# A four-layer Mamba image network on one core: B, C and step sizes of a segment from one projection, and another end for the last image

## The chip, the cores and the metric

The kernel runs on one core of a Trainium2 chip. The metric is the device time of one execution in microseconds (us); the time before is the median of three runs. Engines are named as in the profile: PE is TensorE (PEld its weight loads), DVE is VectorE, ACT is ScalarE, POOL is GpSimd, SP is SyncE, which here only issues DMAs. [...]

## The reference

Four images of 64 x 64 pixels (4096 tokens each) with 96 channels pass four layers. Each layer is a mixer and a feed-forward network, both with a residual, behind layer norms. The mixer of layer 0 is a gated scan; those of layers 1 to 3 are a selective scan in four directions (rows, columns, and both backwards), with 192 channels, 16 states and step sizes of rank 6. What matters here, cut from one of them:

```python
xc = silu(depthwise_conv(x @ in_proj_w.T ...))           # 192 channels
xs = stack([rows, columns, rows backwards, columns backwards])
x_dbl = einsum('bkdl,kcd->bkcl', xs, x_proj_w)            # 6 + 16 + 16 numbers per token
dts, Bs, Cs = split(x_dbl, [R, R + N], axis=2)            # step sizes, B, C
delta = softplus(einsum('bkrl,kdr->bkdl', dts, dt_w) + dt_b)
h = exp(delta * A) * h + delta * u * B                    # per channel and state, over 4096 tokens
y = sum over states of h * C, plus Ds * u                 # then the four directions are added,
out = (layer_norm(y) * silu(z)) @ out_proj_w.T            # normalised, gated and projected
```

The feed-forward network quantises its operands to eight bits and its sums to f16: `relu(q(x W1 + b1))`, then `W2`.

## The kernel before

**Scans.** Layers 1 to 3 of the four images are twelve stages, run one after the other (`scans`). A stage has two directions in time (d), four segments of 1024 tokens in each, and three chunks of 128 partitions (64 channels of each of two orders, rows and columns). Every chunk has 16 states, so a stage has 384 tiles of 128 x 1024 and the kernel 4608. A tile k with state n goes through all engines in a fixed order that the program writes out: SP broadcasts the row of C from a DRAM scratch (`c_rows`, c <- cs); ACT makes the decay (`decays`, da); PE broadcasts the row of B into two PSUM banks (`b_rows`, bc <- bs, sel); DVE multiplies it by du in place (bc <- du, bc) and scans (h <- da, carry, bc); POOL multiplies by C (`times_c`, c <- h, c), one tile later; PE adds the states up in PSUM (`accumulate`, acc), three tiles later. B is needed as bf16 for that broadcast and is kept as three bf16 parts, 32 rows each, that add up to the f32 number; `sel` adds them.

**What runs beside.** Between a tile's DVE product and its scan the program calls `beside`, which advances three generators by a step each: the preparation of the next chunk (`prepare_chunk`: dt_proj, softplus, delta, du), that of the next segment (`next_segment`, `prepare_segment`), and the job of the next stage, the work between two scans of an image (`between`: joining the orders, norm, gating, out_proj, feed-forward, and, for the next layer, norm, in_proj and convolution in strips of 512 tokens). A generator yields where it wants a tile's pause; `yield True` asks for a free bank, and is held up while none is free. There are two single banks (tag `ps`), shared by all three. A `Job` advances by a credit of `rate` steps per tile: 1.65 for a job that the next stage needs, 2.6 for the ends of the first three images, which run in the last two stages. Each engine executes its instructions in the order in which the program issued them (`InOrder`).

**`prepare_segment`** begins at tile n = 4 of a segment's chunk 1, for the next segment. For both halves of 512 columns it projects u (three matmuls over the three chunks) to 108 rows: B three times, rows 0 to 95, and the 12 step-size rows. ACT copies the step sizes to `rows` and B to bf16 in `bs`, 96 rows at once. DVE takes the remainder, `rem = ps - bs`, from PSUM, again 96 rows, and ACT writes rows 32 to 95 of it as bf16 into `bs`. POOL then subtracts the second part from rows 64 to 95, which leaves the third. After that a second projection of the same u, with 32 columns of weights, makes C (x_proj_c), which ACT copies over `rows[0:32]`, and SP stores it to `cs`. The step sizes must be there when chunk 2 begins, else the program drains the segment's generator at that place (`sg.steps`); all of it must be there at n = 13 of chunk 2.

**Norms.** A layer norm's inverse root is Exp(-0.5 Ln(v)), refined by five small POOL instructions. Ln and Exp lie in different tables of ACT. A norm that has been measured is put on `pending`; `logarithms()` takes all of those at once. In a job it is called when no generator can go on for `patience` steps.

**The last image's end** runs alone behind the scans: `Job(between(images[-1], 3, dst), patience=1).finish()`, at the rate of 1.4, on the two single banks. Eight strips pass join (y_t, four joins of eight program matmuls), mixer (y_c, out_proj) and feed-forward (ff_xt, ff_h, ff_y).

Lines: `wide` and `bank` 117 to 128, `Job` 708 to 738, `prepare_segment` 763 to 809, `beside` and the tile loop 985 to 1050, pools and jobs 1285 to 1303, the weights' layout 1335 to 1355. In the trace nearly every instruction is on line 78, the wrapper that keeps the order, so it is read by tile names.

Of the kernel before, what the change touches and what calls it, by code (L numbers as in the profile page):

```python
# [10 lines left out]
F32 = mybir.dt.float32  # L11
# [4 lines left out]
ALU = mybir.AluOpType  # L16
# [5 lines left out]
NS = 16  # L22
DI = 192
R = 6
HID = 4 * C
T = 1024
MM = 512
# [9 lines left out]

NB3 = 96
NC2 = 2 * NS
XPW = NB3 + 2 * R + NC2  # L40
W_IN = 0
W_OUT = W_IN + 6 * 128
W_CW = W_OUT + 2 * C
# [5 lines left out]
W_XP = W_LN + 4  # L49
W_SSM = W_XP + 6 * XPW  # L50

# [48 lines left out]
def metaformer(ctx: ExitStack, tc: tile.TileContext, x, l0_ab, l0_rest, ssm, ffn, out):  # L100
    nc = tc.nc
    pe, act, dve, pool, sp = (
        InOrder(tc, e) for e in (nc.tensor, nc.scalar, nc.vector, nc.gpsimd, nc.sync)
    )
# [4 lines left out]
    pbc = ctx.enter_context(tc.tile_pool(name="pbc", bufs=2, space=bass.MemoryType.PSUM))  # L109

    def sb(bufs, tag, shape, dtype=F32):
        return pools[bufs].tile(shape, dtype, tag=tag, name=tag)

    def const(name, shape, dtype=F32):
        return pools[1].tile(shape, dtype, name=name)

    def wide():
        return pbc.tile([128, T], F32, tag="bc", name="bc")


    banks = {"free": 2, "back": 0}

    def bank(name):
        banks["free"] -= 1
        return pbc.tile([128, MM], F32, tag="ps", name=name)

    def release():
        banks["back"] += 1

    def settle():  # L130
        banks["free"] += banks["back"]
        banks["back"] = 0
# [27 lines left out]
    for k in range(2):  # L160
        p = slice(64 * k, 64 * k + 64)
# [9 lines left out]
    for n in range(NS):  # L171
        for k in range(2):
            at = NS * k + n
# [19 lines left out]
    for layer in range(4):  # L193
# [8 lines left out]
        b = const(f"b_{layer}", [128, 3 + C])  # L202
# [35 lines left out]
    pending = []  # L238
# [36 lines left out]
    class Weights:  # L275
# [17 lines left out]
        def load_xp(self):  # L293
            if self.xp is None:
                self.xp = sb(1, "xp", [128, 6 * XPW])
                sp.dma_start(out=self.xp, in_=ssm[self.layer - 1, :, W_XP:W_SSM])
# [411 lines left out]
    class Job:  # L708
# [23 lines left out]
                    logarithms()  # L732
                    self.waited = 0

        def finish(self):
            while not self.done:
                self.step()
                settle()


# [22 lines left out]
    def prepare_segment(item, sg):  # L763

        xp = weights[item.layer].xp
        m = NB3 + 2 * R

        def project(ps, a, b, k):

            for c in range(3):  # L770
                o = (3 * item.d + c) * XPW
                cols = slice(k * MM, (k + 1) * MM)
                pe.matmul(
                    ps[0 : b - a],
                    xp[:, o + a : o + b],
                    sg.us[c][:, cols],
                    start=c == 0,
                    stop=c == 2,
                )
                if c:  # L780
                    yield

        sg.rows = sb(1, "rows", [128, T])
        for k in range(2):
            cols = slice(k * MM, (k + 1) * MM)
            ps = bank("x_proj_b")
            yield from project(ps, 0, m, k)

            bs = sg.bs[:, cols]
            act.copy(sg.rows[NB3:m, cols], ps[NB3:m])  # L790
            sg.steps = k == 1
            act.copy(bs, ps[0:NB3])
            yield
            rem = sg.rows[0:NB3, cols]
            dve.tensor_tensor(rem, ps[0:NB3], bs, ALU.subtract)
            release()
            yield
            for p in (32, 64):
                act.copy(bs[p : p + 32], rem[p : p + 32])
            yield k == 0  # L800
        pool.tensor_tensor(sg.bs[64:96], sg.rows[64:96], sg.bs[64:96], ALU.subtract)
        for k in range(2):
            cols = slice(k * MM, (k + 1) * MM)
            yield True
            ps = bank("x_proj_c")
            yield from project(ps, m, m + NC2, k)
            act.copy(sg.rows[0:NC2, cols], ps[0:NC2])
            release()
        sp.dma_start(out=sg.cs, in_=sg.rows[0:NC2])

    def prepare_chunk(item):

# [37 lines left out]
    def next_segment(items):  # L850

        sg = load_segment(items[0])
        for i in items:
            i.sg = sg
        yield
        yield
        yield True
        yield from prepare_segment(items[0], sg)

    def scans(stages, jobs, pac):  # L860
# [11 lines left out]
        for i in items[:3]:  # L872
            i.sg = sg
        drain(Chain(prepare_segment(items[0], sg), True))
        drain(Chain(prepare_chunk(items[0]), True))
        tiles = [(i, n) for i in items for n in range(NS)]
# [27 lines left out]
        def b_rows(k):  # L904
            i, n = tiles[k]
            b = live[k, "b"] = wide()
            for half in range(2):
                cols = slice(half * MM, (half + 1) * MM)
                pe.matmul(
                    b[:, cols], sel[:, n, :], i.sg.bs[:, cols], start=True, stop=True  # L910
                )
# [138 lines left out]
    def gated(images, job, pac):  # L1050
# [134 lines left out]
        def project(t):  # L1185

            st, i = t["st"], t["i"]
            t["ab"] = wide()
            for kind in range(2):
                pe.matmul(  # L1190
                    t["ab"][:, kind * MM : (kind + 1) * MM], block(kind, i), st.xn, start=True, stop=True
                )
# [92 lines left out]
    images = [Image() for _ in range(NB)]  # L1285
    for i, im in enumerate(images):
        im.src = x[i * L : (i + 1) * L, :]
        im.dst = out[i * L : (i + 1) * L, :]
    with tc.tile_pool(name="pl0", bufs=1, space=bass.MemoryType.PSUM) as pl0:
        gated(images, Job(between(images[0], 0), 2.6, patience=1), pl0)  # L1290
    stages = [(im, layer) for layer in range(1, 4) for im in images]
    jobs = []
    for at in range(len(stages)):
        jobs.append([])
        if at + 1 < len(stages):
            im, layer = stages[at + 1]
            jobs[-1].append(Job(between(im, layer - 1), 1.65))

        for im in {10: images[:2], 11: images[2:3]}.get(at, ()):
            jobs[-1].append(Job(between(im, 3, im.dst), 2.6))  # L1300
    with tc.tile_pool(name="pac", bufs=1, space=bass.MemoryType.PSUM) as pac:
        scans(stages, jobs, pac)
    Job(between(images[-1], 3, images[-1].dst), patience=1).finish()

# [24 lines left out]
def _chunks(v):  # L1331

    v = v.reshape(2, 2, DI, -1)
    v = [np.concatenate([v[:, o, c : c + 64] for c, o in halves], 1) for halves in CHUNKS]
    return np.stack(v, 1).transpose(2, 0, 1, 3)


def _scan(in_w, conv_w, conv_b, xp_w, dt_w, dt_b, A_logs, Ds, ln_w, ln_b, out_w):
    w = np.zeros((128, W_SSM), np.float32)
    twice = np.r_[128:DI, 128:DI]  # L1340

    xp = np.zeros((128, 2, 3, XPW), np.float32)
    m = NB3 + 2 * R
    for d in range(2):
        for chunk, halves in enumerate(CHUNKS):
            for k, (ch, order) in enumerate(halves):
                t = xp_w[2 * d + order].T[ch : ch + 64]
                v = xp[64 * k : 64 * k + 64, d, chunk]
                for s in range(3):
                    v[:, 32 * s + NS * order : 32 * s + NS * order + NS] = t[:, R : R + NS]  # L1350
                v[:, NB3 + R * order : NB3 + R * order + R] = t[:, :R]
                v[:, m + NS * order : m + NS * order + NS] = t[:, R + NS :]
    w[:, W_XP:W_SSM] = xp.reshape(128, -1)
    t = in_w.T
    w[:C, W_IN : W_IN + 448] = np.concatenate([t[:, :128], t[:, twice], t[:, DI:]], 1)
    dt = np.zeros((2 * R, 2, 3, 128), np.float32)
    for d in range(2):
        for chunk, halves in enumerate(CHUNKS):
            for k, (ch, order) in enumerate(halves):
                t = dt_w[2 * d + order].T  # L1360
                dt[R * order : R * order + R, d, chunk, 64 * k : 64 * k + 64] = t[:, ch : ch + 64]
    w[NB3 : NB3 + 2 * R, W_IN:W_OUT] = dt.reshape(2 * R, -1)
    w[:, W_OUT : W_OUT + C] = out_w.T[:128]
    w[:64, W_OUT + C : W_CW] = out_w.T[128:]
    taps = conv_w.reshape(DI, 9)
    w[:, W_CW : W_CW + 9] = taps[:128]
    w[:64, W_CW + 9 : W_CB] = np.concatenate([taps[128:, 0:3], taps[128:, 6:9]], 1)
    w[64:, W_CW + 9 : W_CW + 12] = taps[128:, 3:6]
    w[:, W_CB:W_DTB] = np.stack([conv_b[:128], conv_b[twice]], 1)
    w[:, W_DTB:W_AL] = _chunks(dt_b[..., None]).reshape(128, -1)  # L1370
    w[:, W_AL:W_DS] = _chunks(A_logs.reshape(4, DI, NS)).reshape(128, -1)
    w[:, W_DS:W_LN] = _chunks(Ds.reshape(4, DI, 1)).reshape(128, -1)
    w[:, W_LN : W_LN + 2] = np.stack([ln_w[:128], ln_b[:128]], 1)
    w[:64, W_LN + 2 : W_XP] = np.stack([ln_w[128:], ln_b[128:]], 1)
    return w
# [46 lines left out]
```

## Time and profile before

| | us |
|---|---|
| median of three runs | 19681.59 |
| lowest and highest of them | 19680.81, 19689.28 |
| the profiled execution's own time | 19688.32 |
| span of its profile | 19686.5 |
| of that: layer 0, to the first scan of layer 1 | 1817.2 |
| scans of layers 1 to 3 | 17576.5 |
| end of the last image, behind the last scan | 292.8 |
| mean granted clock of PE | 0.815 of full |

Busy over the span: DVE 90%, PE 83%, POOL 79%, ACT 62%. Times in the profile are from the start of the span. "Idle before" is the time an engine stood still ahead of an instruction, with what ended it: `DVE bc <- PE bc` means that the DVE product of a tile waited for the PE broadcast into its tile. A PE matmul of the program with f32 operands is two records in the trace. A view of windows gives each engine's busy time in a stretch, in the order PE, PEld, DVE, ACT, POOL, and the granted clock of PE; a timeline gives start, duration, engine and operation.

### The profile page before, as it was taken

The numbers are of one execution on the slowest core, as the hardware profiler recorded it, in microseconds if no ns is written. First come the engines' busy times: TensorE is split into PE (matmuls) and PEld (weight loads), VectorE is DVE, ScalarE is ACT, GpSimd is POOL, SyncE is SP. The second block draws the span as 40 slices with busy tenths as digits, with TensorE's granted clock in tenths as the row PEclk, the third lists the DMA queues.
The fourth block names the chain that finished last, engine by engine and source line by source line (L and its number), as shares of the span: only waits on it lengthen the run. The fifth ranks groups of instructions, "written<-read, shape, count | busy, mean of one in ns | idle before, by whom it ended". The sixth has DMA issues, their size and how long they took to land. (4 is left out here: it accounts for less than half of the span.)

```text
span 19686.5 us, 224801 instructions
## 1 busy us (share of the span) xinstructions
PE 16267.7 (83%) x70400; PEld 4750.9 (24%) x70400; DVE 17666.9 (90%) x13768; ACT 12256.8 (62%) x19331; POOL 15495.8 (79%) x10086
## 2 busy tenths in 40 slices
PE   8998787787888887787887888787888888888876
PEld 3332121121122222222222222222222222222223
DVE  6757999999999999999999999999999999998884
ACT  4544665665665665665666666666666666666664
POOL 3435888888888888888888888888888888878884
PEclk9998787787887797797797787797887787787886
DMA  2213676666676667666666676666666666676663
GB/s 52 50 48 87 169 185 168 170 187 164 171 189 173 166 184 182 168 185 178 170 188 176 170 186 172 170 188 174 171 186 172 170 189 174 171 187 169 165 176 89
DMA packets 1269876, 3192.65 MB, mean 162 GB/s; under 512 B 440336, under 2 KB 440560, under 8 KB 1262544
## 3 DMA queue, kind: packets, MB, share of 16 engines
q1 hardware_dynamic: 1268688, 3178.27, 61.5%
q8 instruction: 568, 9.31, 0.2%
q14 instruction: 620, 5.08, 0.1%
HBM read 2818.81 MB, written 308.28 MB: 159 GB/s over the span
## 5 line engine op out<-in xcount | busy, mean ns | idle before, releaser
L78 POOL TENSOR_TENSOR c<-h,c 128x1024 f32<-128x1024 f32 (+1 forms) x4992 | 11334.8, 2277 | 3377.8 <-DVE h L78 1478.0
L78 DVE TENSOR_TENSOR_SCAN h<-da,carry,bc 128x1024 f32<-128x1024 f32 x4608 | 10795.4, 2343 | 530.3 <-POOL c L78 17.0
L78 PE MATMUL acc<-c,twice 64*64 64x512 f32 x36864 | 6215.7, 751 | 20.1 <-POOL c L78 20.0
L78 ACT ACTIVATE da<-delta,decay 128x1024 f32<-128x1024 f32 x4608 | 5280.9, 1147 | 1491.5 <-DVE h L78 1475.6
L78 DVE TENSOR_TENSOR bc<-du,bc 128x1024 f32<-128x1024 f32 x4608 | 5565.6, 1208 | 488.4 <-PE bc L78 461.6
L78 PE MATMUL bc<-bs,sel 96*128 96x512 bf16 x9216 | 3384.4, 455 | 2343.3 <-DVE h L78 2235.9
L78 ACT COPY carry<-h 128x1 f32<-128x1 f32 x3456 | 649.5, 188 | 3374.5 <-DVE h L78 3368.7
L78 PEld LDWEIGHTS <-sel 96*128 96x128 bf16 x9216 | 552.2, 101 | 7301.0 <-DVE h L78 5519.2
L78 PEld LDWEIGHTS acc<-c,twice 64*64 64x64 f32 x36864 | 1130.7, 153 | 2799.4 <-issue 1860.2
L78 ACT ACT_TABLE_LOAD x1155 | 1481.9, 1283 | 36.5 <-DVE mv L78 20.3
L78 PE MATMUL conv<-pad,tap_lo 128*128 128x512 f32 x1728 | 906.5, 634 | 0.0
L78 PE MATMUL dt_proj<-rows,w 12*128 12x512 f32 x1152 | 826.5, 804 | 6.4 <-ACT delta L78 6.4
L78 ACT ACTIVATE du<-e,ones 128x1024 f32<-128x1024 f32 x576 | 659.3, 1145 | 199.3 <-POOL delta L78 194.5
L78 POOL TENSOR_TENSOR delta<-delta,du 128x1024 f32<-128x1024 f32 x288 | 679.8, 2361 | 72.0 <-ACT du L78 70.3
L78 PE MATMUL x_proj_b<-u,xp 128*108 128x512 f32 x1152 | 687.6, 713 | 46.4 <-DMA xp<-in_ssm 15.5
L78 PE MATMUL x_proj_c<-u,xp 128*32 128x512 f32 x1152 | 642.0, 672 | 76.1 <-ACT rows L78 67.0
L78 POOL TENSOR_TENSOR e<-e,du 128x1024 f32<-128x1024 f32 x288 | 679.8, 2360 | 2.4 <-ACT du L78 2.4
L78 ACT ACTIVATE c<-c,l_bias 128x512 f32<-128x512 f32 x384 | 263.6, 686 | 670.5 <-PE c L78 665.9
L78 POOL TENSOR_TENSOR du<-delta,u 128x1024 f32<-128x1024 f32 x288 | 680.4, 2363 | 0.1
L78 POOL TENSOR_TENSOR delta<-delta,e 128x1024 f32<-128x1024 f32 x288 | 678.8, 2357 | 0.1
L78 PE MATMUL conv<-pad,tap_hi 128*128 128x512 f32 (+1 forms) x1152 | 601.8, 624 | 0.6 <-ACT u L78 0.5
L78 DVE TENSOR_TENSOR_SCAN h<-da,l_carry,bc 128x512 f32<-128x512 f32 x384 | 491.4, 1280 | 41.9 <-DVE bc L78 2.3
(152 smaller groups left out, 15200.8 us busy)
## 6 DMA issues: line engine op xcount, KB each, us to landing
c<-cs SPq DMA_DIRECT2D x9216, 256.0 KB, 4.2
u<-u SPq DMA_DIRECT2D x288, 512.0 KB, 6.7
y<-y SPq DMA_DIRECT2D x1152, 128.0 KB, 3.2
y<-y SPq DMA_DIRECT2D x144, 512.0 KB, 6.8
xr<-x SPq DMA_DIRECT2D x224, 192.0 KB, 5.1
u<-u SPq DMA_DIRECT2D x288, 128.0 KB, 3.6
pad<-y SPq DMA_DIRECT2D x288, 128.0 KB, 4.9
z<-zl SPq DMA_DIRECT2D x96, 256.0 KB, 2.0
```

Of the source, the lines that this page charges most:

```text
L78: ins = f(*a, **k).ins
```

## The change

**In a segment's preparation** there is one projection to 108 rows: B in rows 0 to 31, C in 32 to 63, zeros in 64 to 95, step sizes in 96 to 107. ACT copies all 108 rows from PSUM to `rows`, then the first part of B, 32 rows, to bf16, and the bank is released. Two steps later DVE takes the remainder of the 32 rows from `rows` and `bs`, both in SBUF, into `rows[64:96]`; ACT copies it to `bs` twice; POOL makes the third part as before. C goes from `rows[32:64]` to DRAM. The second projection and its two copies are gone.

**Job rate**: 1.58 in place of 1.65 for jobs that the next stage needs.

**The last image's end**: the two wide PSUM tiles (four banks) come from a pool of their own that is closed behind the scans. The end then has six single banks, a rate of 3, and `eager=True`: `logarithms()` is called after every step that left something pending.

```diff
-XPW = NB3 + 2 * R + NC2
+XPW = NB3 + 2 * R
...
-        def finish(self):
+        def finish(self, eager=False):
             while not self.done:
                 self.step()
+                if eager and pending:
+                    logarithms()
                 settle()
...
     def prepare_segment(item, sg):
         xp = weights[item.layer].xp
-        m = NB3 + 2 * R
-        def project(ps, a, b, k):
-            for c in range(3):
-                o = (3 * item.d + c) * XPW
-                cols = slice(k * MM, (k + 1) * MM)
-                pe.matmul(ps[0 : b - a], xp[:, o + a : o + b], sg.us[c][:, cols], ...)
-                if c:
-                    yield
-        sg.rows = sb(1, "rows", [128, T])
+        rows = sg.rows = sb(1, "rows", [128, T])
         for k in range(2):
             cols = slice(k * MM, (k + 1) * MM)
-            ps = bank("x_proj_b")
-            yield from project(ps, 0, m, k)
+            ps = bank("x_proj")
+            for c in range(3):
+                o = (3 * item.d + c) * XPW
+                pe.matmul(ps[0:XPW], xp[:, o : o + XPW], sg.us[c][:, cols], ...)
+                if c:
+                    yield
             bs = sg.bs[:, cols]
-            act.copy(sg.rows[NB3:m, cols], ps[NB3:m])
+            act.copy(rows[0:XPW, cols], ps[0:XPW])
             sg.steps = k == 1
-            act.copy(bs, ps[0:NB3])
-            yield
-            rem = sg.rows[0:NB3, cols]
-            dve.tensor_tensor(rem, ps[0:NB3], bs, ALU.subtract)
+            act.copy(bs[0:32], ps[0:32])
             release()
             yield
+            yield
+            rem = rows[64:96, cols]
+            dve.tensor_tensor(rem, rows[0:32, cols], bs[0:32], ALU.subtract)
+            yield
             for p in (32, 64):
-                act.copy(bs[p : p + 32], rem[p : p + 32])
+                act.copy(bs[p : p + 32], rem)
             yield k == 0
-        pool.tensor_tensor(sg.bs[64:96], sg.rows[64:96], sg.bs[64:96], ALU.subtract)
-        for k in range(2):
-            cols = slice(k * MM, (k + 1) * MM)
-            yield True
-            ps = bank("x_proj_c")
-            yield from project(ps, m, m + NC2, k)
-            act.copy(sg.rows[0:NC2, cols], ps[0:NC2])
-            release()
-        sp.dma_start(out=sg.cs, in_=sg.rows[0:NC2])
+        sp.dma_start(out=sg.cs, in_=rows[NC2 : 2 * NC2])
+        pool.tensor_tensor(sg.bs[64:96], rows[64:96], sg.bs[64:96], ALU.subtract)
...
-            jobs[-1].append(Job(between(im, layer - 1), 1.65))
+            jobs[-1].append(Job(between(im, layer - 1), 1.58))
...
-    Job(between(images[-1], 3, images[-1].dst), patience=1).finish()
+    with tc.tile_pool(name="pend", bufs=6, space=bass.MemoryType.PSUM) as pend:
+        banks.update(free=6, back=0, pool=pend)
+        Job(between(images[-1], 3, images[-1].dst), 3, patience=1).finish(eager=True)
```

More of the change, by code (lines that the diff above doesn't have):

```diff
@@ L115, in const @@
         return pools[1].tile(shape, dtype, name=name)
+    wides = []
     def wide():
-        return pbc.tile([128, T], F32, tag="bc", name="bc")
-    banks = {"free": 2, "back": 0}
+        return wides[0].tile([128, T], F32, tag="bc", name="bc")
+    banks = {"free": 2, "back": 0, "pool": pbc}
     def bank(name):
         banks["free"] -= 1
-        return pbc.tile([128, MM], F32, tag="ps", name=name)
+        return banks["pool"].tile([128, MM], F32, tag="ps", name=name)
     def release():
@@ L765, in prepare_segment @@
         xp = weights[item.layer].xp
-        m = NB3 + 2 * R
-        def project(ps, a, b, k):
+        rows = sg.rows = sb(1, "rows", [128, T])
+        for k in range(2):
+            cols = slice(k * MM, (k + 1) * MM)
+            ps = bank("x_proj")
             for c in range(3):
                 o = (3 * item.d + c) * XPW
-                cols = slice(k * MM, (k + 1) * MM)
                 pe.matmul(
[L774 to L778, printed above, removed]
+                    ps[0:XPW], xp[:, o : o + XPW], sg.us[c][:, cols], start=c == 0, stop=c == 2
                 )
@@ L781, in project @@
                     yield
-        sg.rows = sb(1, "rows", [128, T])
-        for k in range(2):
-            cols = slice(k * MM, (k + 1) * MM)
-            ps = bank("x_proj_b")
-            yield from project(ps, 0, m, k)
             bs = sg.bs[:, cols]
-            act.copy(sg.rows[NB3:m, cols], ps[NB3:m])
+            act.copy(rows[0:XPW, cols], ps[0:XPW])
             sg.steps = k == 1
-            act.copy(bs, ps[0:NB3])
-            yield
-            rem = sg.rows[0:NB3, cols]
-            dve.tensor_tensor(rem, ps[0:NB3], bs, ALU.subtract)
+            act.copy(bs[0:32], ps[0:32])
             release()
             yield
+            yield
+            rem = rows[64:96, cols]
+            dve.tensor_tensor(rem, rows[0:32, cols], bs[0:32], ALU.subtract)
+            yield
             for p in (32, 64):
-                act.copy(bs[p : p + 32], rem[p : p + 32])
+                act.copy(bs[p : p + 32], rem)
             yield k == 0
-        pool.tensor_tensor(sg.bs[64:96], sg.rows[64:96], sg.bs[64:96], ALU.subtract)
-        for k in range(2):
-            cols = slice(k * MM, (k + 1) * MM)
-            yield True
-            ps = bank("x_proj_c")
-            yield from project(ps, m, m + NC2, k)
-            act.copy(sg.rows[0:NC2, cols], ps[0:NC2])
-            release()
-        sp.dma_start(out=sg.cs, in_=sg.rows[0:NC2])
+        sp.dma_start(out=sg.cs, in_=rows[NC2 : 2 * NC2])
+        pool.tensor_tensor(sg.bs[64:96], rows[64:96], sg.bs[64:96], ALU.subtract)
     def prepare_chunk(item):
@@ L1288, in metaformer @@
         im.dst = out[i * L : (i + 1) * L, :]
[L1289 to L1296, printed above, removed]
-            jobs[-1].append(Job(between(im, layer - 1), 1.65))
[L1299 to L1302, printed above, removed]
-    Job(between(images[-1], 3, images[-1].dst), patience=1).finish()
+    with tc.tile_pool(name="pbig", bufs=2, space=bass.MemoryType.PSUM) as wides_pool:
+        wides.append(wides_pool)
+        with tc.tile_pool(name="pl0", bufs=1, space=bass.MemoryType.PSUM) as pl0:
+            gated(images, Job(between(images[0], 0), 2.6, patience=1), pl0)
+        stages = [(im, layer) for layer in range(1, 4) for im in images]
+        jobs = []
+        for at in range(len(stages)):
+            jobs.append([])
+            if at + 1 < len(stages):
+                im, layer = stages[at + 1]
+                jobs[-1].append(Job(between(im, layer - 1), 1.58))
+            for im in {10: images[:2], 11: images[2:3]}.get(at, ()):
+                jobs[-1].append(Job(between(im, 3, im.dst), 2.6))
+        with tc.tile_pool(name="pac", bufs=1, space=bass.MemoryType.PSUM) as pac:
+            scans(stages, jobs, pac)
+    with tc.tile_pool(name="pend", bufs=6, space=bass.MemoryType.PSUM) as pend:
+        banks.update(free=6, back=0, pool=pend)
+        Job(between(images[-1], 3, images[-1].dst), 3, patience=1).finish(eager=True)
 def _layer0(W_in, b_in, W_out, b_out, gamma, beta):
@@ L1342, in _scan @@
     xp = np.zeros((128, 2, 3, XPW), np.float32)
-    m = NB3 + 2 * R
     for d in range(2):
@@ L1348, in _scan @@
                 v = xp[64 * k : 64 * k + 64, d, chunk]
-                for s in range(3):
-                    v[:, 32 * s + NS * order : 32 * s + NS * order + NS] = t[:, R : R + NS]
+                v[:, NS * order : NS * order + NS] = t[:, R : R + NS]
+                v[:, NC2 + NS * order : NC2 + NS * order + NS] = t[:, R + NS :]
                 v[:, NB3 + R * order : NB3 + R * order + R] = t[:, :R]
-                v[:, m + NS * order : m + NS * order + NS] = t[:, R + NS :]
     w[:, W_XP:W_SSM] = xp.reshape(128, -1)
```

## The prediction, made before the changed kernel ran

> **What bounds the kernel now.** I read the busy shares first, then windows by part, then DVE's groups and waits, last the timeline around the step that changes. By part (layer 0, scans, end of the last image):
>
> ```profile
> 0.00:1817.20 1817.20, 1597.55 (x4170) 622.65 (x4170) 1170.96 (x1706) 822.35 (x1715) 694.94 (x1192) 0.92 0.21 52
> 1817.20:19393.70 17576.50, 14493.66 (x65366) 4019.14 (x65366) 16465.70 (x11919) 11330.46 (x17389) 14733.69 (x8757) 0.81 0.67 176
> 19393.70:19686.50 292.80, 176.49 (x867) 109.15 (x864) 30.22 (x144) 104.03 (x227) 67.19 (x137) 0.50 0.19 45
> ```
>
> In the scans DVE is busy 16466 of 17577 us (94%), POOL 84%, PE 82%: DVE sets the time, and an instruction or a wait on it counts in full. DVE's waits there, and two rows of instructions:
>
> ```profile
> DVE bc L78 <- PE bc L78: 461.6, 271, 20.7
> DVE rows L78 <- ACT bs L78: 28.6, 15, 3.9
> ...
> L78 DVE TENSOR_TENSOR rows<-x_proj_b,bs x192: 671/677/689, 1788.7 to 19146.5; 96x512 f32<-96x512 f32 x192
> L78 PE MATMUL x_proj_c<-u,xp x1152: 592/593/1062, 1789.9 to 19173.5; 128*32 128x512 f32 x192
> ```
>
> PE's backlog costs DVE 461.6 us in 271 waits, and the remainder of B 28.6 us. In the end part no engine is full; PE leads with 176 of 293 us at half its clock. The timeline around one remainder, DVE and then POOL:
>
> ```profile
> 10041.50 1.23 DVE L78 TENSOR_TENSOR bc<-du,bc 128x1024 f32<-128x1024 f32 x1 [0.42 <-PE bc L78]
> 10042.64 0.68 DVE L78 TENSOR_TENSOR rows<-x_proj_b,bs 96x512 f32<-96x512 f32 x1
> 10043.24 2.33 DVE L78 TENSOR_TENSOR_SCAN h<-da,carry,bc 128x1024 f32<-128x1024 f32 x1
> ...
> 10042.26 4.67 POOL L78 TENSOR_TENSOR c<-h,c 128x1024 f32<-128x1024 f32 x2
> ```
>
> The remainder sits between product and scan, and POOL is in the middle of c <- h, c: that product is released by the scan before, as DVE's own next product is. Three DVE instructions, each with one tensor in PSUM and at most one in SBUF (and a column of carries), run through it undisturbed.
>
> [...] 182 of the 192 remainders began inside a POOL instruction, and all took 671 to 689 ns. [...] no DVE instruction with two SBUF tensors met a POOL product. The change makes one. [...] The trace has 1283, but what follows the load starts 1.3 us after its start[...]
>
> **The change part by part.** All against the profiled execution's own 19688.3 us, which is 6.7 above the median of 19681.6.
>
> *Second projection removed.* 1152 records of 593 ns or more, 642 us of PE and 192 ACT copies of 560 ns, 107 us. ACT (62%) is no bound. PE's part counts only where it delays bc. I followed each DVE wait for bc of over 0.2 us back along PE to its last pause of over 0.4 us, at most 25 us, and took the x_proj_c time in that run, capped by the wait: 68 us in all. They stand in chunk 2 at n = 4 and 5, beside dt_proj. Jobs that were refused a bank then will move in: in the built program a job ends some 10 tiles earlier in a stage although its rate is lower. I take 55; bounds 25 and 90 (all the waits at those two n are 104).
>
> *Remainder, its length.* 32 rows in place of 96, the same 512 columns[...]. The copy of 108 rows takes what that of 12 did (578 ns), by columns.
>
> *Remainder, its old wait.* It now comes two steps behind ACT's copies, not one, so the 28.6 us go: -29 (0 to -30).
>
> *Remainder, its new wait.* By the order of the built program it stands at n = 11 of chunk 1 (91 of 95 segments) and n = 1 of chunk 2 (95), behind the tile's product. At those places of the trace of before I read what was left of the running POOL instruction when the DVE product ended: mean 1.28 us, median 1.37, 178 of 191 times c <- h, c, hardly ever nothing. If the lock holds, 192 x 1.28 = +246 us, on DVE, with nothing that hides it: the scan is queued behind, behind that all of DVE, and POOL's next c waits for the scan. Bounds: 0 (no contention) and 2.36 us, if POOL's next product goes first (it follows within 0.15 us in 83%), x192 = 453. I take 246: DVE has asked before that product is dispatched. While DVE waits PE works off its backlog; PE's waits in the three tiles behind those places, capped at 1.28 each, are 53 us, 32 of them at the n = 4 already counted: -15.
>
> *Moved steps.* Step sizes are ready a pump later; the built program drains for them 5 times of 96, one step each: up to 2 us each, I take 0, since da is two tiles ahead. The `cs` store moves from n = 8 to 10 of chunk 2 up to n = 4, on an SP queue whose next reader of it stands at n = 14. POOL's subtraction (2.12 us) goes from n = 2 to n = 4; bs is read a chunk later. Table loads rise from 1155 to 1191: 36 x 1.28 = 46 us of ACT, some 10 of them in the end. No job is forced at its due tile in either program. All 0, within -15 to +20.
>
> *The end.* By the built order, each strip's round is now y_t 19 of 32, y_c, y_t, ff_xt, y_t, y_c, y_t, ff_h, out_proj, ff_h, out_proj, ff_y, one strip per round. From an out_proj's end the norm's chain (DVE 1.7 us, ACT's two norm steps, Ln, load and Exp 2.3, POOL 1.4, ACT's normalising 1.9) takes some 7.3; ff_y and 19 y_t fill about 6.9 of it on PE. So a round is PE's own work: (176.5 - 1.7)/8 = 21.8 us at the clock of 0.50, where the x <- xr, out_proj of before are 194.2/7 = 27.7 apart. First strip: out_proj ended 36.3 us after the first y_t, since 64 y_t and both strips' norms came first; now 9.7 to the last copy, 8.3 to the normalised tile, then y_c to out_proj with 16 y_t between: 30.2. Second round 22.5 (its norms come late), five of 21.8, the eighth without y_t 18.3; then one feed-forward, 18.1 as the trace has it, and the store's 3.1, in place of two in a row (35.0). With the 27.3 us ahead of the first y_t, which stay: 27.3 + 30.2 + 22.5 + 109 + 18.3 + 21.2 = 228.5 for 292.8, -64. Bounds -35 (a wait that I missed in each round) and -95[...].
>
> Sum: -55 + 2.5 - 29 + 246 - 15 - 64 = +85: 19773 for the profiled execution, 19766 for the median.
>
> **The rivals.** *No contention* (ends faster): the lock doesn't bite for these operands. Then +246 and -15 fall away: -55 + 2.5 - 29 - 64 = -145.5, 19536. For it: no trace here shows the lock. [...] It decides from a wait of (145.5/192) = 0.76 us per remainder: below that the change gains. *Shared, not locked*: the remainder is slowed to about double, [...] +132 in place of +246, no pause to catch up: -13, 19668, no change. *POOL goes first*: the wait is 1.28 + 2.36 where POOL has more queued. At a third of the remainders, 64 x 2.36 = +151 more, 19917[...].
>
> **How the numbers follow.** Lock as priced 0.57, POOL first 0.03, shared 0.14, none 0.26. The likeliest gives 19766; its own range, from the bounds of the other terms taken together (some 60 to 70 us either way, not all at one end), is 19705 to 19835. The range that should hold 8 in 10 reaches to the rival without contention: 19520 to 19820, leaving out about 0.10 below (the faster half of that rival, a larger gain in the end) and 0.08 above. 0.2% is 39 us, about what a measurement of this kernel can tell from no change. Slower by more than that: 0.47 of the lock case, all of POOL first, 0.01 of the shared case: 0.51. Faster by more: 0.25 of the rival without contention and 0.04 of the shared one: 0.29. Within: the rest, 0.20.
>
> **What would show it.** In the profile of after: in front of or within rows <- rows, bs some 1.3 us more than before, ending with a POOL c, and DVE's idle time in the scans up by 100 us or more[...]. DVE's waits for bc down from 461.6 to about 400, hardly any at n = 4 and 5 of chunk 2. The end 220 to 240 us, x <- xr, out_proj about 22 apart. Wrong: if the remainder runs through c <- h, c, the sign is wrong; if bc's waits don't fall, freed PE time was taken by jobs.

## The result, and the profile after

| | before | after |
|---|---|---|
| median, us | 19681.59 | 19728.74 |
| lowest and highest of 17 runs each | 19651.91, 19700.97 | 19696.47, 19756.45 |
| ratio of the times | | 1.0023, 95% interval 1.0016 to 1.0031 |
| span of the profile | 19686.5 | 19719.6 |
| mean granted clock of PE | 0.815 | 0.794 |

The kernel became slower by 47 us, 0.23%. The forecast was 19766, slower; it was 37 us too high.

The windows by part, after (layer 0, scans, end; columns as before: PE, PEld, DVE, ACT, POOL, clock, DMA share, GB/s):

```profile
0.00:1800.00 1800.00, 1580.51 (x4158) 618.63 (x4158) 1171.29 (x1705) 820.53 (x1713) 692.88 (x1192) 0.93 0.21 52
1800.00:19503.70 17703.70, 14293.60 (x64226) 3974.11 (x64226) 16780.41 (x11919) 11230.33 (x17227) 14763.23 (x8757) 0.78 0.67 174
19503.70:19719.60 215.90, 163.04 (x868) 108.75 (x864) 29.80 (x145) 113.51 (x235) 67.32 (x137) 0.51 0.26 61
```

Against before, the scans are 127 us longer, the end 77 shorter, and layer 0 is 17 shorter. Layer 0 is scatter: it took 1798 to 1813 us in every profile below, whichever edit was in, so the 1817 of before was a long one. In the scans DVE is busy 315 us longer with the same 11919 instructions; 287 of that is one group, below. PE is busy only 200 us less, although 1140 records have gone, and its clock fell from 0.81 to 0.78.

DVE's waits in the scans of after, and then the row of the remainder by its tile name (durations in ns, lowest, median and highest):

```profile
DVE bc L78 <- PE bc L78: 362.4, 250, 22.6
...
DVE rows L78 <- ACT bs L78: 2.0, 4, 0.7
```

```profile
L78 DVE TENSOR_TENSOR rows<-rows,bs x192: 682/1882/8531, 1774.2 to 19276.0; 32x512 f32<-32x512 f32 x192
```

The waits for bc fell by 99 us and the remainder's old wait for ACT from 28.6 to 2. What grew is the remainder itself, from a median of 677 ns to one of 1882. **The new wait is inside the instruction's own duration**: it is no idle time, no view of waits names it, and it looks like 287 us more work (415.7 us in the scans for 128.7). The sign that the forecast had named, DVE's idle time up by 100 us or more, is therefore not there: that idle time fell from 1111 us to 923. What it waited for shows in the timeline, DVE and then POOL:

```profile
10101.80 1.21 DVE L78 TENSOR_TENSOR bc<-du,bc 128x1024 f32<-128x1024 f32 x1
10103.04 1.88 DVE L78 TENSOR_TENSOR rows<-rows,bs 32x512 f32<-32x512 f32 x1
10104.95 2.35 DVE L78 TENSOR_TENSOR_SCAN h<-da,carry,bc 128x1024 f32<-128x1024 f32 x1
...
10102.02 2.36 POOL L78 TENSOR_TENSOR c<-h,c 128x1024 f32<-128x1024 f32 x1 [1.25 <-DVE h L78]
```

POOL's product ends at 10104.38, the remainder at 10104.92: 0.54 us after it. Over all 190 remainders in the scans, what was left of the running POOL instruction was 1.30 us on average, and the rest of the duration 0.55.

The longest one, in the same order:

```profile
7680.37 8.53 DVE L78 TENSOR_TENSOR rows<-rows,bs 32x512 f32<-32x512 f32 x1
...
7680.19 1.25 POOL L78 TENSOR_TENSOR u<-u,zh 64x512 f32<-64x512 f32 x1
7681.42 4.64 POOL L78 TENSOR_TENSOR c<-h,c 128x1024 f32<-128x1024 f32 x2
7686.02 2.33 POOL L78 TENSOR_TENSOR delta<-delta,e 128x1024 f32<-128x1024 f32 x1
```

Here POOL was busy with a job's u <- u, zh, and three instructions stood behind it. The remainder began to wait at 7680.37, and all three still went ahead of it: it ended 0.55 us after the last. There are 16 such cases, all at chunk 1, n = 11; seven let one further instruction go first, six two and three three, 28 of 2.33 us in all, some 65 us.

In the end the x <- xr, out_proj stand some 20 us apart, evenly but for the last, 17 us behind the seventh (three of the eight are shown); before, distances of 15 to 19 us and of 41 took turns:

```profile
19602.28 0.56 DVE L78 TENSOR_TENSOR x<-xr,out_proj 128x384 f32<-128x384 f32 x1 [4.90 <-issue]
19621.49 0.56 DVE L78 TENSOR_TENSOR x<-xr,out_proj 128x384 f32<-128x384 f32 x1 [4.41 <-POOL hq L78]
19641.01 0.55 DVE L78 TENSOR_TENSOR x<-xr,out_proj 128x384 f32<-128x384 f32 x1 [4.90 <-issue]
```

### The profile page after: what moved, and what is told of

Read it like the earlier page. It is cut to its first block, busy times and chain, and to the rows that moved or that the text cites. A ratio compares the mean times of both kernels' runs of the same rounds, so it can differ in the third digit from the quotient of the medians.

```text
span 19719.6 us, 222333 instructions
## 1 busy us (share of the span) xinstructions
PE 16037.2 (81%) x69248; PEld 4701.5 (24%) x69248; DVE 17981.5 (91%) x13768; ACT 12164.4 (62%) x19175; POOL 15523.4 (79%) x10086
## 5 line engine op out<-in xcount | busy, mean ns | idle before, releaser
L78 PE MATMUL acc<-c,twice 64*64 64x512 f32 x36864 | 6396.7, 772 | 7.7 <-POOL c L78 7.6
L78 PE MATMUL bc<-bs,sel 96*128 96x512 bf16 x9216 | 3488.1, 468 | 2718.6 <-DVE h L78 2623.5
L78 ACT ACT_TABLE_LOAD x1191 | 1528.1, 1283 | 63.8 <-DVE h L78 26.9
L78 PE MATMUL x_proj<-u,xp 128*108 128x512 f32 x1152 | 699.6, 725 | 50.2 <-ACT ff_h L78 12.6
L78 PE MATMUL y_t<-ident,pad 128*128 128x128 f32 (+1 forms) x1536 | 414.2, 359 | 124.3 <-DMA pad<-y 119.2
```

The lines of the kernel that those rows point to most:

```text
L78: ins = f(*a, **k).ins
```

## The experiments

The theory after this reading: the lock on the two SBUF operands (with them the remainder stands until POOL's running instruction has ended, as at 10104.38 above) costs some 230 us net, the end gives some 75, and the removed projection the rest. Its rivals: the longer remainder is due to its partitions (rows 0 to 31 in, 64 to 95 out) and not to SBUF; the lower job rate, which had no term of its own in the forecast, gives what was put down to the projection; the end gains by its banks, or by its logarithms, alone. Each kernel was timed in five rounds against the kernel before; "ratio" is to that, with its 95% interval.

| | kernel | median, us | ratio | scans | end |
|---|---|---|---|---|---|
| 1 | after, remainder from PSUM | 19513.39 | 0.9916 (0.9902 to 0.9929) | 17492.1 | 215.7 |
| 2 | before, remainder from SBUF | 19908.66 | 1.0114 (1.0101 to 1.0128) | 17812 | 292.6 |
| 3 | before, new end | 19607.39 | 0.9958 (0.9944 to 0.9971) | 17566.2 | 216.2 |
| 4 | after, remainder ahead of the product | 19625.74 | 0.9971 (0.9960 to 0.9982) | 17603 | |
| 5 | 1, job rate 1.65 | 19650.25 | 0.9985 (0.9977 to 0.9993) | 17643.2 | 214.8 |
| 6 | after, remainder on POOL | 19410.35 | 0.9860 (0.9845 to 0.9875) | 17387.3 | 215.7 |
| 7 | 3 without the logarithms at once | 19671.26 | 0.9991 (0.9983 to 0.9999) | 17585.5 | 288.5 |
| 8 | 3 on two banks | 19619.96 | 0.9963 (0.9950 to 0.9975) | 17580.2 | 233.8 |
| 9 | before, job rate 1.58 | 19587.28 | 0.9958 (0.9945 to 0.9970) | 17510.1 | |
| 10 | 6, job rate 1.52 | 19434.79 | 0.9884 (0.9867 to 0.9900) | 17408.6 | |
| 11 | 1, each projection twice | 19616.59 | 0.9973 (0.9963 to 0.9983) | 17604.4 | 214.9 |
| 12 | before, new end, rate 1.58 | 19514.19 | 0.9920 (0.9906 to 0.9933) | 17478.5 | 215.0 |

**1. The remainder's first operand from PSUM**, the bank released behind it; all else as in after.

```diff
             act.copy(bs[0:32], ps[0:32])
-            release()
             yield
             yield
             rem = rows[64:96, cols]
-            dve.tensor_tensor(rem, rows[0:32, cols], bs[0:32], ALU.subtract)
+            dve.tensor_tensor(rem, ps[0:32], bs[0:32], ALU.subtract)
+            release()
```

> The changed kernel, but the remainder of B takes its first operand from the PSUM bank, which is held two steps longer; one SBUF input in place of two, output and place as in the changed kernel. Lock theory: the remainder falls from a mean of 2.19 us to about 0.68 and DVE wins back 192 x 1.5 = 288 us; less up to 40 us where the longer hold of a bank keeps a job back: 19440 to 19490 for the 19729 of the changed kernel, 0.988 to 0.990 of the kernel before. Rival, that the write to other partitions (from rows 0 to 31 to rows 64 to 95) or the new place in the tile order costs the time: the remainder stays at about 2 us, time within 20 us of 19729.

```profile
L78 DVE TENSOR_TENSOR rows<-x_proj,bs x192: 681/682/684, 1777.8 to 19059.6; 32x512 f32<-32x512 f32 x192
```

The wait is gone at every one of the 192 places: all took 681 to 684 ns, with one tensor in PSUM, in the same places behind the same products and across the same partitions. The time fell by 215 us. The remainders gave 286, and DVE's idle time in the scans rose by 71, from 923 to 994. So 71 us of other waits are back. Either the lock's pauses had hidden them, or they come from the bank that is held two steps longer here; this run can't tell the two apart. Because of them the time missed the expected range by 23 us.

**2. Only the SBUF operand, put into the kernel before**: ACT copies all 108 rows, and the remainder of 96 rows is taken in place.

```diff
-            act.copy(sg.rows[NB3:m, cols], ps[NB3:m])
+            act.copy(sg.rows[0:m, cols], ps[0:m])
...
-            dve.tensor_tensor(rem, ps[0:NB3], bs, ALU.subtract)
+            dve.tensor_tensor(rem, rem, bs, ALU.subtract)
```

> The kernel before, with one thing of the change: ACT copies all 108 rows to SBUF and the remainder, still 96 rows and in place, takes both operands from SBUF; bank and steps as before. Lock theory: each remainder grows by what POOL has left, 1.3 us and a whole POOL product more where one is queued, +250 to +290 us: 19930 to 19970. Rival, that the cross-partition write or the place does it: no change, 19680. Rival, that PE's backlog hides such a wait: +100 or less.

```profile
L78 DVE TENSOR_TENSOR rows<-rows,bs x192: 673/2003/4841, 1780.6 to 19371.9; 96x512 f32<-96x512 f32 x192
```

The same jump, with input and output on the same partitions: 372.2 us in the scans for 128.7, +244, or 1.28 us each, and +226 us of time. The rival of the partitions falls; two SBUF operands are enough. The time is 21 us below the expected range, as the remainders grew a little less than expected and DVE's idle time fell by 11 us. At 10 places one further product of POOL went first.

**3, 7, 8. The end**, put alone into the kernel before (3: the diff's lines in `finish`, `wide`, `bank` and the last image's job); then without `eager=True` (7); then with `bufs=2` and `free=2` (8).

> The kernel before, with the changed end of the last image alone (six banks, rate 3, logarithms at once), segments and job rate as before. By the trace of after the end is 216 us for 293: -77, so 19600 to 19610. If part of those 77 us belongs to what the scans left behind, less.

> The kernel before with six banks and a rate of 3 in the last image's end, but logarithms called only when nothing can go on, as before. Splits the 75 us of the end: my working put a round at PE's own work once norms are known a strip earlier, so most should be the early logarithms: this run keeps 10 to 35 of the 75 us, 19645 to 19675. Rival, that two banks held the strips back: it keeps 50 or more, 19630 or less.

> The kernel before with logarithms at once and a rate of 3 in the last image's end, but on two banks. If early logarithms are what counts, it keeps 45 us or more of the 75: 19640 or less; if the banks do, 25 or less, 19655 or more.

The windows of the end part in 3, 7 and 8:

```profile
19374.90:19591.10 216.20, 164.25 (x864) 109.71 (x864) 29.75 (x144) 113.77 (x235) 67.30 (x137) 0.51 0.26 61
```

```profile
19384.20:19672.70 288.50, 171.35 (x865) 107.88 (x864) 30.22 (x144) 104.02 (x227) 67.16 (x137) 0.51 0.19 46
```

```profile
19380.90:19614.70 233.80, 167.81 (x868) 109.86 (x864) 29.73 (x145) 116.09 (x237) 67.42 (x137) 0.51 0.24 57
```

The new end is worth 75 us of time on the old projection, and 77 of the end part on either. All three times lie in their expected ranges. Six banks and the higher rate without the logarithms at once keep only 4 us of the end part (288.5 for 292.8). The logarithms at once on two banks, with the higher rate, give 59; the other four banks add the last 18. In 8 the x <- xr, out_proj stand 22 us apart, in after 20. That PE's next strip waits there for one of the two banks is likely, but I did not trace it.

**4. The remainder ahead of the tile's product** in place of behind it, where POOL was expected to be between two products.

```diff
+    def ahead_of_product():
+        for out_, x_, y_ in early:
+            dve.tensor_tensor(out_, x_, y_, ALU.subtract)
+        early.clear()
...
             rem = rows[64:96, cols]
-            dve.tensor_tensor(rem, rows[0:32, cols], bs[0:32], ALU.subtract)
+            early.append((rem, rows[0:32, cols], bs[0:32]))
...
+            ahead_of_product()
             dve.tensor_tensor(b, i.du, b, ALU.mult)
```

> The changed kernel, but the remainder, with its two SBUF inputs, is issued ahead of the tile's product and not behind it. There POOL's next product is released by the same scan that lets DVE go on: in the trace of before POOL had 0.51 us left at that place at n = 11 of chunk 1 and 0.07 us at n = 1 of chunk 2. Lock theory (who starts first holds it): the remainder falls to about 0.6 to 1.1 us, the time by 200 to 240 us to 19490 to 19530, and the POOL product of those tiles starts about 0.6 us later. Rival, that two SBUF inputs are slow beside POOL whoever starts first[...]: the remainder stays above 1.2 us, and the time above 19640.

At 19625.74 it missed the expected times of the theory and of the rival alike, and it shows two things. At chunk 2, n = 1 the remainder now comes first, and POOL pays (timeline, DVE and then POOL):

```profile
10234.80 2.35 DVE L78 TENSOR_TENSOR_SCAN h<-da,carry,bc 128x1024 f32<-128x1024 f32 x1
10237.18 0.68 DVE L78 TENSOR_TENSOR rows<-rows,bs 32x512 f32<-32x512 f32 x1
10237.79 1.21 DVE L78 TENSOR_TENSOR bc<-du,bc 128x1024 f32<-128x1024 f32 x1
...
10237.28 2.81 POOL L78 TENSOR_TENSOR c<-h,c 128x1024 f32<-128x1024 f32 x1 [0.99 <-PE dt_proj L78]
```

The product of POOL that began 0.10 us after the remainder took 2.81 us for 2.36: it stood still while the remainder ran. In all, 118 products of POOL began within such a remainder, and they took 2.54 to 2.84 us, with a median of 2.80. So the wait works both ways, and the instruction that others wait for keeps its length: the remainder 0.68 us here, POOL's product 2.36 us in after, at 10102.02. That both are slowed while both run is excluded. At chunk 1, n = 11 the remainder still averages 2.05 us and up to 8.65: there POOL is behind by a job's work at that tile, and neither of the two places tried was free.

**5. The version of 1 at the old job rate**, and **9. the kernel before at the new one.**

```diff
-                jobs[-1].append(Job(between(im, layer - 1), 1.58))
+                jobs[-1].append(Job(between(im, layer - 1), 1.65))
```

> The first experiment (remainder from PSUM, one projection, new end) with the job rate put back from 1.58 to 1.65. If the lower rate carried part of what the freed PE time is worth (DVE's waits for bc, 462 us before and 384 in the first experiment), those waits rise by 20 us or more and the time with them, 19535 to 19560; if the gain is the removed projection's alone, it stays within 15 us of 19513.

> The kernel before with one number changed, the layer jobs' rate of 1.65 set to 1.58 as in the kernel after; two of the eleven stages then push the last five steps of a job at their end. If it is the lower rate that gains and not the removed projection: the PSUM version at rate 1.58 stood 137 us under the same at 1.65, so 19,545 to 19,620 here, with waits of DVE for B's broadcast about 100 us under before's 461.6. If the lower rate only pays because the removed projection left PE room for it: 19,660 to 19,700, with those waits unchanged.

The waits of DVE for bc in the scans, first 1, then 5:

```profile
DVE bc L78 <- PE bc L78: 383.9, 245, 19.7
```

```profile
DVE bc L78 <- PE bc L78: 509.9, 285, 23.0
```

At the old rate the merged projection, even without the lock, is 43 us slower than 3, which has the same end, rate and a remainder from PSUM; its waits for bc are higher than before's 461.6. Its time is 137 us above 1, far more than either expectation had it. And the rate alone, with both projections in place, gains 87 us, as expected; the waits for bc fell by 28 us only, where about 100 had been expected. The remainder waits 26 us less for ACT, and DVE's idle time in the scans is 74 us lower in all (1111 to 1036):

```profile
DVE bc L78 <- PE bc L78: 433.9, 297, 20.2
...
DVE rows L78 <- ACT bs L78: 3.1, 6, 0.6
```

**12. Old projection, new end, new rate**: the partner of 1, which differs from it in the projection and in where the remainder stands.

```diff
-                jobs[-1].append(Job(between(im, layer - 1), 1.65))
+                jobs[-1].append(Job(between(im, layer - 1), 1.58))
```

(on top of 3)

> The kernel before with the new end and the rate 1.58, and with the old projection, remainder from PSUM included: it stands beside the version of after with its remainder from PSUM (19,513 us), which has the same end and rate and the merged projection. If the merged projection gains nothing by itself, at this rate as at 1.65: 19,500 to 19,525 (before 19,681.6, less 87 for the rate alone and 75 for the end alone, gives 19,519). If the 640 us of PE time that it frees are worth the forecast's 55 us and more: 19,560 to 19,600.

19514.19 beside 19513.39: **at this rate the second projection cost nothing that these runs can tell**, to within some 25 us. DVE's waits for bc are 32 us lower without it (415.6 and 383.9), those for out_proj 20 higher. The windows of the scans, first 12, then 1:

```profile
1807.20:19285.70 17478.50, 14418.71 (x65366) 3990.53 (x65366) 16472.55 (x11919) 11352.51 (x17412) 14722.49 (x8757) 0.81 0.67 177
```

```profile
1803.60:19295.70 17492.10, 14291.13 (x64226) 3974.16 (x64226) 16497.74 (x11919) 11199.53 (x17192) 14718.01 (x8757) 0.78 0.67 176
```

607 us of x_proj_c have gone (602 in the scans), and PE is busy 128 us less. The reason stands in PE's groups, 12 and then 1 (busy, mean ns, idle before and what ended it):

```profile
L78 PE MATMUL acc<-c,twice 64*64 64x512 f32 x36864 | 6184.4, 747 | 2.9 <-POOL c L78 2.9
L78 PE MATMUL bc<-bs,sel 96*128 96x512 bf16 x9216 | 3388.9, 456 | 2400.0 <-DVE h L78 2303.6 <-DMA c<-cs 79.6 <-ACT ff_h L78 5.5
```

```profile
L78 PE MATMUL acc<-c,twice 64*64 64x512 f32 x36864 | 6399.8, 772 | 3.7 <-POOL c L78 3.7
L78 PE MATMUL bc<-bs,sel 96*128 96x512 bf16 x9216 | 3490.6, 468 | 2558.1 <-DVE h L78 2415.5 <-DMA c<-cs 117.3 <-DMA z<-zl 11.9
```

The same matmuls take 25 and 12 ns longer each, 317 us over these two groups, as PE's clock is granted less (0.81 in 12, 0.78 in 1). The clock records of the two traces show where. They have only two values, the whole clock and half of it. One acc takes on average 612 or 613 ns at the whole clock and 1083 or 1084 at half, in both runs; only the share of records at half differs, 26% in 12 and 31% in 1. In the scans the clock is at half for 6523 us in 12 and for 7625 in 1, and 655 of the 1102 us more stand in the tiles n = 3 to 9 of chunk 2, where x_proj_c had run.

**11. The version of 1 with every projection computed twice**, the second over the first. It puts the PE work back, and adds two steps to each half of a segment.

```diff
-            for c in range(3):
+            for c in (0, 1, 2, 0, 1, 2):
```

> The kernel after with the remainder from PSUM (19,513 us), and every projection computed twice into the same bank, the second time over the first: 1,152 more matmuls, about 700 us of PE at 608 ns each, and no other change but two more steps of preparation for each half of a segment. If the time that the removed projection freed on PE is what gains: waits of DVE for B's broadcast rise from 385 to 430 or more and the time to 19,560 to 19,620. If PE's granted clock takes back what the removed matmuls freed (it fell from 0.815 to about 0.79 when they went): the clock rises again to 0.81, the other matmuls shorten to their lengths of before, and the time stays at 19,500 to 19,540.

```profile
L78 PE MATMUL acc<-c,twice 64*64 64x512 f32 x36864 | 6326.0, 763 | 10.4 <-POOL c L78 10.4
L78 PE MATMUL x_proj<-u,xp 128*108 128x512 f32 x2304 | 1219.2, 657 | 35.4 <-DMA xp<-in_ssm 15.3 <-ACT u L78 14.8 <-ACT zl L78 1.5
```

The clock rose from 0.792 to 0.810, acc shortened from 772 to 763 ns and bc from 468 to 462: part of the way back to 12. PE's busy time rose by 253 us for 540 us of added projections. So the clock does what was expected of it. The time, up by 103 us, and the 519 us of waits for bc are what was expected of the other reading, though, and the trace shows why. Of these waits 174 us stand at chunk 2, n = 1, where 1 has none. With two steps more for each half the step sizes are not ready when chunk 2 begins, so the program drains the rest of the second half there. In all 95 segments 8 or 12 records of x_proj then run in one piece ahead of a bc, where 1 has no piece longer than 4 (PE, then DVE):

```profile
10256.71 3.68 PE L78 MATMUL x_proj<-u,xp 128*108 128x512 f32 x8
10260.23 0.60 PE L78 MATMUL bc<-bs,sel 96*128 96x512 bf16 x2
...
10260.86 1.23 DVE L78 TENSOR_TENSOR bc<-du,bc 128x1024 f32<-128x1024 f32 x1 [1.14 <-PE bc L78]
```

Everywhere else the waits for bc fell, from 384 to 345. So the run shows what work in one piece ahead of a bc costs; that spread PE work costs nothing is read from 12 and 1.

**6, 10. The remainder on POOL**, which is where the lock leaves nothing to wait for; then at a still lower rate.

```diff
-            dve.tensor_tensor(rem, rows[0:32, cols], bs[0:32], ALU.subtract)
+            pool.tensor_tensor(rem, rows[0:32, cols], bs[0:32], ALU.subtract)
```

> The changed kernel, with the remainder computed by POOL in place of DVE, same operands and place in the order. DVE loses 192 instructions and never meets the lock; POOL gains 192 of about 1.2 us, 235 us on its 15523. Lock theory: time of the first experiment less what DVE saved, 192 x 0.68 = 130 us, as far as POOL's queue (84% busy in the scans, full at n = 11 of chunk 1) lets it: 19390 to 19480. Rival, that POOL is the bound at those places: DVE's scans and PE's accumulation then wait for later products, 19510 or more.

> The kernel after with the remainder on POOL (19,410 us) and the layer jobs' rate set from 1.58 to 1.52, at which the jobs still end before each stage does. If less crowding of PE by the jobs' steps goes on paying at half the slope seen from 1.65 to 1.58 (137 us for 0.07): 19,350 to 19,390. If 1.58 has already taken what there is: 19,395 to 19,440.

```profile
L78 POOL TENSOR_TENSOR rows<-rows,bs x192: 1144/1148/1168, 1777.6 to 18967.3; 32x512 f32<-32x512 f32 x192
```

It takes 1148 ns there, at most 1168, 1.7 times as long as on DVE, and costs 220 us of POOL, which is busy 86% of the scans, DVE 94%; DVE loses 131 us of work, of which 103 show against 1. 19410.35 is 318 us below after and 271 below before, and the best of all. The rate of 1.52 gives nothing on top (24 us more, the intervals overlap), as expected if 1.58 had taken what there was.

## Why the forecast was right, and where it was not

The terms, and what the runs put in their place:

| step | forecast | measured | from |
|---|---|---|---|
| second projection, remainder's length and old wait | -55 + 2.5 - 29 | -1 | 1 against 12 |
| job rate | no term | -87 | 9 |
| remainder's new wait, with PE's catching up | +246 - 15 | +215 | after against 1 |
| the end | -64 | -75 | 3 |
| sum | +85 | +52 | the change itself: +47 |

The four measured parts, each uncertain by some 25 us, add up to the whole within 5. That is a weak check: before, 12, 1 and after follow each other, so it tests only that rate and end add up (-87 and -75 apart, -167 together in 12).

**The new wait was right in mechanism and place, and its net size by errors that cancel.** The sign hung on it. The pauses came to 286 us for 246 and the catching up to 71 for 15, so the net was 215 for 231; in 2 the time rose by 226. The residue of POOL's instruction was 1.30 us where 1.28 had been read off the trace of before. The lock stands in these runs: at the same place the remainder took 682 ns with one tensor in PSUM (1) and a median of 1882 with two in SBUF (after), and POOL's product was held up in its turn, a median of 2.80 us for 2.36 (4). "No contention" and "shared, not locked" are both excluded. Who asks first does not always go first: at 16 places DVE began to wait before one to three of POOL's queued instructions began, and they still went ahead. One reading was off without consequence: in the trace of before 190 of the 192 remainders began inside a POOL instruction, and not 182. A remainder that has waited ends 0.55 us after its releaser and not 0.68, so the average pause is less than the residue by 0.13; against that, POOL's queue goes first.

**That POOL goes first was given 0.03 and happens**, at 16 of 190 remainders and for some 65 us; priced at a third of them it would have been 151. The reason given against it, that DVE had asked before the product was dispatched, is wrong: at 7680.37 DVE had asked, and three instructions that began later went ahead. What kept it rare is probably that POOL mostly has nothing queued, as its next c needs the scan that stands behind the remainder.

**PE's catching up** was put at -15. Between after and 1 DVE's idle time differs by 71 us: 22 ahead of bc, 22 ahead of x <- xr, out_proj, 18 for the DMA of xr, and smaller ones. Between before and 2, with pauses of the same kind, it differs by 11, nearly all ahead of bc. So the size held in 2 and was too small by 56 us in after. Since 1 also holds a bank two steps longer, how much of the 71 us is PE catching up stays open.

**The second projection was priced at the right place and for the wrong cause.** The 104 us of waits at n = 4 and 5 of chunk 2 did fall to 46. But in 9, with both projections, they fell to 47, and in 5, with the one projection at the old rate, only to 83: most of it was the rate. Nor do the waits of one place give the total: in 9 those of chunk 1 rose from 100 to 179 us. The step that failed is the one where I set the lower rate aside ("although its rate is lower") and took PE time ahead of a wait for what the wait is worth. Two things stand against it. When 607 us of matmuls go, the clock falls from 0.821 to 0.792 and the rest lengthen by most of it, so that PE is busy only 128 us less; and in 11 the 8 or 12 records of x_proj in one piece ahead of a bc made 174 us of waits at one place where 1 has none. That the lower rate gains by shorter pieces is likely, and not traced. The removed projection gained 0 and the rate 87, where 82 had been put on the projection with the remainder's length and old wait: that these two sizes agree is luck, and the forecast came near by it.

**The remainder's old wait** did go (28.6 to 2), but the rate alone takes it to 3.1, so it does not count for the move. Its length grew by 5 ns (682 for 677), 1 us in all; the +2.5 of the forecast rested on no trace.

**The end** was worth 11 to 13 us more than forecast. A round was taken for PE's own work at a clock of 0.50, 21.8 us. The x <- xr, out_proj stand 20 apart, and PE's work in the part fell from 176.5 to 163.0 with a clock of 0.51. The mechanism holds: from the second of them to the seventh PE is busy for 96.9 of 99.0 us, where it was for 112.0 of 161.7 before. So a round is PE's own work, 19.4 us of it. The "first strip" and the tail I did not test apart.

**Moved steps**, at 0, were not measured apart: they are part of the -1 between 1 and 12. Table loads rose to 1191 as counted, with a mean of 1283 ns before and after; ACT is busy 62% of the span in both, and what the 36 more cost in time was not shown.

**The clock, and what stays open.** The clock was lower in 1 than in 12 and 11, which have 1152 more matmul records of the projection: 0.792 for 0.821 and 0.810. There are 655 us more at half the clock where x_proj_c had run (1 beside 12), and 664 us less of it at n = 1 to 4 of chunk 2, in and behind the doubled second half (11 beside 1). What sets it was not traced.

## What to carry to other kernels

Before you move a DVE operand from PSUM to SBUF to release a bank early, look at what POOL is doing at that place: with two SBUF operands the remainder waited here for POOL's running instruction, and at 16 of 190 places for one to three more that were queued. That was 1.5 us on 0.7 us of work on average, and the wait shows as duration. A small elementwise step on the engine that bounds may be cheaper on the engine that it would have to wait for, though it is slower there (1148 ns on POOL for 682 on DVE, and 103 us less time than 1). Do not price removed PE work by its busy time alone: here 607 us of it made PE busy only 128 us less, at a clock of 0.792 for 0.821. Test it with and without, with all else the same, and give a changed rate or pacing constant a term of its own.

## What was not expected of the hardware

- PE's granted clock fell from 0.821 to 0.792 when 1152 matmul records were taken away, and rose again to 0.810 when as many were added (12, 1, 11); acc took 747, 772 and 763 ns. Of the 1102 us more at half the clock, 655 stand where the removed matmuls had run.
- A remainder that waited for POOL did not always get in between POOL's queued instructions: at 16 of 190 places one to three of them went first, and the longest such remainder took 8.53 us.
- The wait lengthens the record of the waiting instruction on either side: 682 to a median of 1882 ns on DVE, 2.36 to a median of 2.80 us on POOL.
